# Sixteen rows of x put together in stage 2 instead of transposed in stage 3, another way for the last core plane, and another order of the opening

## The chip, the core and the metric

The kernel runs on one core of one Trainium2 chip. The metric is device time in microseconds (us) of the whole program; three runs of the kernel before gave 3287.86, 3288.17 and 3288.30. Everything is float32. The engines are named as in the profile: PE is TensorE's matrix product and PEld its weight load, DVE is VectorE, ACT is ScalarE, POOL is GpSimd, and SP is SyncE, which here only issues transfers. A float32 product is two passes through TensorE, so a product counts as two PE instructions.

## The reference

A "triangle" layer is followed by a gated layer, on x of 384 x 384 positions (i, j) with 128 channels. Cut to what matters:

```python
z = layernorm(x, norm_g, norm_b)                       # over channels
left  = (z @ Wl + bl) * sigmoid(z @ Wlg + blg)
right = (z @ Wr + br) * sigmoid(z @ Wrg + brg)
core  = einsum('ikh,jkh->ijh', left, right)            # per hidden channel h: a 384x384x384 product
zo    = layernorm(core, onorm_g, onorm_b) @ Wout + bout
x1    = x + sigmoid(x @ Wg + bg) * zo                  # end of layer 0

l   = x1 @ W_left + b_left + x1 @ W_eq + b_eq
rs  = sum over j of (x1 @ W_right + b_right)           # one vector per row i
o   = (l * rs * sigmoid(x1 @ W_gate + b_gate)) @ W_out + b_out
out = layernorm(o + x1, ln_scale, ln_bias)
```

## The kernel before

The work runs in three stages, one after another, with tensors in device memory between them. `seq` keeps all instructions in the order of the program text, so each engine's order is written out by hand.

**Opening (0 to 11 us).** x's first chunk is loaded on SP in two halves with `load_chunk`, the side weights W (128 x 514 with the norm's columns, into `stage`) and their bias row are loaded on ACT's queue. `fold` turns the norm's gain and shift into the weights: `busy(2)` (line 150) issues two products that serve nothing but to occupy TensorE, POOL makes a matrix m1 (lines 159, 160), and for each half of the columns a full product (line 163) and a bias product (line 164), whose operands are one row high (`avg[0:1]`, `brow`), are summed in PSUM. `weights` (line 171, DVE) makes the folded matrix `wz` of it, and `first_step` (line 288) transposes the first rows of normalised x.

**Stage 1 (to 1130 us)** takes x in chunks of 8 rows i by 128 positions k. DVE computes the layer norm's moments, POOL subtracts (`z`, line 262), TensorE transposes (line 271) and multiplies by `wz` (line 323, 128x512), ACT takes the sigmoid (line 332), DVE the product (line 334). Three things go to memory: left and right, by hidden channel, to `lr_d`; the transposed z to `xt_d` (channel, i, block, position); and the subtracted part to `nd_d`. The two sum to x, transposed: x^T of row i is `xt_d[:, i]` plus `nd_d[i]` on every channel.

**Stage 2 (1130 to 1874 us)** is a loop over the 128 hidden channels h. `load_h` brings left and right of one h in two transfers (lines 93 and 94, 768 and 256 KB) into one of three buffers; it is issued for h+3 when TensorE has finished h. `fill(h+1)` copies the right factors to a dense tile `rr` on POOL, one h ahead (lines 468 to 475; the first of the two copies of loaded data, line 474, is 128x768). Nine products (line 493) give three planes of core in PSUM. ACT copies them out (`ct`, line 502) and squares them (line 503), DVE sums both over h (lines 504 and 505) for the second layer norm, and SP stores the planes to `core_d` (line 509, 576 KB). One h takes 5.81 us. The last h has its own sequence: its first plane has a PSUM bank of its own, is copied out first (line 511), stored in two pieces (16 rows and the rest, lines 513 and 514), and the variance, its root (line 425), reciprocal (line 429) and a Newton step (lines 439 to 441) make `r`, the reciprocal deviation for rows 0 to 127. The rest of the planes is copied at line 517 and stored at line 522; POOL's queue stores `r` to `rstd_d` (line 525).

**Stage 3 (1874 to 3287 us)** goes row by row through a written pipeline of steps t. For each row: the gate product `pg` (line 621) and its sigmoid (line 623), the scaled core `cs` (rows 0 to 3 on DVE, line 655, with r spread over the partitions by the product `pb`, line 654; other rows on POOL, line 657, with the loaded `rt`), the product `pr` (line 666), two DVE steps to x1 (lines 667 and 669), two products of layer 1 (lines 683 and 684) with a sigmoid and a product behind them, the output product (lines 695 and 696), the layer norm over channels and the store. All of it needs x transposed. For rows 16 and up, `load_x` reads `nd_d`, spread over the partitions (line 568), and `add_x` adds `xt_d` to it by an accumulating transfer on POOL's queue (line 576). For rows 0 to 15, `load_x` reads x itself (line 562), and `front` transposes each row in three pieces (line 632) and copies it out of PSUM on ACT (line 636) or, for rows 4 to 8, on DVE (line 634); the gate product of a row lags its transposes by L = 4 rows. `load_core` brings core rows in groups of four (line 586); that of the first group is in two transfers, the last 16 channels being the second, and has no `rt`; the others add `rt` (line 590).

SP issues in the order of the text: x of rows 0 to 11, core of rows 0 to 3 (two pieces), x of rows 12 to 15, core and rt of rows 4 to 7, and so on. An issue that waits holds up all that stand behind it in its queue.

Of the kernel before, what the change touches and what calls it, by code (L numbers as in the profile page):

```python
# [8 lines left out]
F32 = mybir.dt.float32  # L9
# [10 lines left out]
def triangle_then_gated_row_kernel(ctx: ExitStack, tc: tile.TileContext, a: dict, out: bass.AP):  # L20
# [9 lines left out]

    nc = tc.nc
    x = a["x"].rearrange("b i j c -> (b i) j c")
    y = out.rearrange("b i j c -> (b i) j c")
# [7 lines left out]
    KEEP = 2  # L43
    RG = 4
    A = 9
    L = 4
    TR = 16

    cpool = ctx.enter_context(tc.tile_pool(name="const", bufs=1))
# [3 lines left out]
    rstd_d = dpool.tile([N, N], F32, name="rstd_d")  # L53
    xt_d = dpool.tile([C, N, NB, P], F32, name="xt_d")
    nd_d = dpool.tile([N, N], F32, name="nd_d")

    def seq(ins):

# [22 lines left out]
    with ExitStack() as ctx2:  # L81
# [17 lines left out]
        with tc.tile_pool(name="p1w", bufs=6, side="right") as wp, \  # L99
# [26 lines left out]
            stage = lrp.tile([P, H, G, 2], F32, tag="lr", name="stage").rearrange("p h i s -> p (h i s)")  # L126

            wst, g0, b0 = stage[:, 0:4 * H], stage[:, 4 * H:4 * H + 1], stage[:, 4 * H + 1:4 * H + 2]
            brow, m1, d = stage[0:1, 5 * H:9 * H], stage[:, 9 * H:10 * H], stage[:, 10 * H:10 * H + 1]
            load(stage[:, 0:4 * H + 2], a["L0_side_W"], nc.scalar)  # L130
            load(brow, a["L0_side_b"].rearrange("(o h) -> o h", o=1), nc.scalar)
            load_chunk(0, slice(4, XR))
            for n in range(1, 4):
                load_chunk(n)
# [1 line left out]
            seq(nc.vector.memset(avg, 1.0 / P))  # L136
            mhalf = const([P, 16], "mhalf")
            seq(nc.vector.memset(mhalf, -0.5))
            ident = const([P, P], "ident")
            make_identity(nc, ident)  # L140

# [5 lines left out]
            def busy(n):  # L147

                for _ in range(n):
                    seq(nc.tensor.matmul(  # L150
                        p0, lhsT=avg, rhs=avg.unsqueeze(1).to_broadcast([P, 4, P]), start=True, stop=True
                    ))

            def fold():

                busy(2)
                seq(nc.gpsimd.tensor_tensor(d, b0, g0, ALU.subtract))
                seq(nc.gpsimd.tensor_tensor(m1, avg, d.to_broadcast([P, P]), ALU.mult))  # L160

                for p, gs in zip((p0, p1), halves):
                    seq(nc.tensor.matmul(p[:, gs], lhsT=m1, rhs=wst[:, gs], start=True, stop=False))
                    seq(nc.tensor.matmul(p[:, gs], lhsT=avg[0:1, :], rhs=brow[:, gs], start=False, stop=True))

            halves = slice(0, 2 * H), slice(2 * H, 4 * H)

# [275 lines left out]
        with tc.tile_pool(name="p2r", bufs=2, side="right", reuse_waits="tile") as rrp, \  # L443
# [14 lines left out]
            def fill(h):  # L458

                if h < H:  # L460
# [15 lines left out]
                    if h == 0:  # L476
                        stay()

            fill(0)
            for h in range(H):  # L480
                fill(h + 1)
                t, rr = loaded2.pop(h), right.pop(h)
                pc = ps.tile([P, NB, 512], F32, tag="pc", name="pc")
                banks = [pc[:, ib, :N] for ib in range(NB)]
                order = [(kb, ib) for kb in range(NB) for ib in range(NB)]
                if h == H - 1:


                    banks[0] = ps1.tile([P, 512], F32, name="pc0")[:, :N]
                    order.sort(key=lambda o: o[1] > 0)  # L490
                    seq(nc.scalar.activation(warm, mhalf[:, 0:1], AF.Sqrt, scale=-1.0))
                for kb, ib in order:
                    seq(nc.tensor.matmul(  # L493
                        banks[ib], lhsT=t[:, kb, ib * P:(ib + 1) * P, 0], rhs=rr[:, kb],
                        start=(kb == 0), stop=(kb == NB - 1),
                    ))

                ct = op.tile([P, NB, N], F32, tag="ct", name="ct")
                sq = qp.tile([P, NB, N], F32, tag="sq", name="sq")
                to = core_d[:, h, :].rearrange("(b p) j -> p b j", p=P)  # L500
                if h < H - 1:
                    seq(nc.scalar.copy(ct, pc[:, :, :N]))  # L502
                    seq(nc.scalar.activation(sq, ct, AF.Square))
                    seq(nc.vector.tensor_add(csum, csum, ct))  # L504
                    seq(nc.vector.tensor_add(csq, csq, sq))
                    load_h(h + 3)

                    queue = nc.sync if h < H - 3 else nc.scalar
                    seq(queue.dma_start(out=to, in_=ct))
                else:  # L510
                    seq(nc.scalar.copy(ct[:, 0], banks[0]))
                    seq(nc.scalar.activation(sq[:, 0], ct[:, 0], AF.Square))
                    seq(nc.scalar.dma_start(out=to[:16, 0], in_=ct[:16, 0]))
                    seq(nc.scalar.dma_start(out=to[16:, 0], in_=ct[16:, 0]))
                    seq(nc.vector.tensor_add(csum[:, 0], csum[:, 0], ct[:, 0]))
# [12 lines left out]
                    seq(nc.gpsimd.tensor_tensor(csq[:, 1:], csq[:, 1:], sq[:, 1:], ALU.add))  # L528
# [5 lines left out]
    with ExitStack() as ctx3:  # L534
# [11 lines left out]
        def work(name, pool=wp):  # L546
            return pool.tile([P, N], F32, tag=name, name=name)

        def work_x(name):

            return lp.tile([P, N], F32, tag="x", name=name)
# [5 lines left out]

        def load_x(i0):

            if i0 < TR:  # L560
                xt = xin[i0] = xp.tile([P, RG, N], F32, tag="xt", name="xn")
                seq(nc.sync.dma_start(
                    out=xt.rearrange("p i (b c) -> p i b c", b=NB),
                    in_=x[i0:i0 + RG].rearrange("i (b p) c -> p i b c", p=P),
                ))
            elif i0 < N:
                xt = xts[i0] = xp.tile([P, RG, N], F32, tag="xt", name="xt")
                seq(nc.sync.dma_start(
                    out=xt.rearrange("p i j -> p (i j)"),
                    in_=nd_d[i0:i0 + RG].rearrange("i j -> (i j)").partition_broadcast(P),  # L570
                ))

        def add_x(i0):
# [7 lines left out]
        def load_core(i0):  # L581
# [33 lines left out]

        def front(f):

            r = rows.get(f - L)
            if r:
                pg = bank("pg")  # L620
                seq(nc.tensor.matmul(pg[:, :N], lhsT=wg0, rhs=r["xT"], start=True, stop=True))  # L621
                gT = r["gT"] = work("gT", fp)
                seq(nc.scalar.activation(gT, pg[:, :N], AF.Sigmoid, bias=bg0))  # L623
            if f < N:
                i0, n = f // RG * RG, f % RG
                if f >= TR:
                    xT = xts[i0][:, n]
                else:
                    xT = work_x("xT")
                    pxt = ps2.tile([P, 512], F32, tag="py", name="pxt") if f < A else bank("pxt")  # L630
                    for s in cols:
                        seq(nc.tensor.transpose(pxt[:, s], xin[i0][:, n, s], ident))
                    if 4 <= f < A:
                        seq(nc.vector.tensor_copy(xT, pxt[:, :N]))
                    else:
# [23 lines left out]
        def layer0(i):  # L659
# [8 lines left out]
            x1T = r["x1T"] = work_x("x1T")  # L668
            seq(nc.vector.scalar_tensor_tensor(
                x1T, pr[:, :N], bout1, r["xT"], ALU.add, ALU.add, accum_out=quad[m]["tot"][:, n:n + 1]  # L670
            ))
# [220 lines left out]
```

## Time and profile before

| what | before |
|---|---|
| three runs, median | 3288.17 us |
| profiled execution, its own time | 3288.61 us |
| its span | 3286.8 us |
| PE busy | 3266.3 us, 99% |
| POOL busy | 2289.6 us, 70% |
| DVE busy | 2491.7 us, 76% |
| ACT busy | 1936.1 us, 59% |
| transfers | 873.70 MB, mean 266 GB/s |

The span runs from the first to the last instruction that the profile shows; the program's own time has some 1.8 us around it. Busy shares are averages over stages that differ: stage 2 and stage 3 each have TensorE busy nearly all the time, while what stands close behind it changes. In rows of the timeline the columns are start, duration, engine, line, operation, tiles and shapes, how many were drawn together, and in brackets how long the engine stood idle before and what released it. In rows of windows they are the stretch and its length, then busy time and instruction count for PE, PEld, DVE, ACT and POOL, then the granted clock of TensorE, the mean busy share of the core's 16 DMA engines, and GB/s.

### The profile page before, as it was taken

The page shows a single profiled execution, that of the slowest core. Times are in us where ns is not written, and L with a number is a line of the kernel's source. Part 1 is how long each engine was busy: PE and PEld are TensorE (multiplying, and loading weights), DVE is VectorE, ACT ScalarE, POOL GpSimd, SP SyncE. Part 2 cuts the span into 40 slices and gives each one's busy share as a digit, 9 for nine tenths or more (in the row PEclk, how much of TensorE's full clock was granted, in tenths as well). Part 3 has the DMA queues.
Part 4 walks back from the last instruction along what each step waited for, and adds up shares of the span by engine and source line. Part 5 has one row for each costly group of instructions (what it writes and reads, how often), then busy time and mean ns, then how long its engine had stood idle before and what let it go on. Part 6 is the DMA issues. An engine that isn't in the chain of part 4 may idle for free.

```text
span 3286.8 us, 48304 instructions
## 1 busy us (share of the span) xinstructions
PE 3266.3 (99%) x12458; PEld 1987.4 (60%) x12458; DVE 2491.7 (76%) x8019; ACT 1936.1 (59%) x4056; POOL 2289.6 (70%) x3299
## 2 busy tenths in 40 slices
PE   9999999999999999999999999999999999999998
PEld 4444444444444566666666666667777777777776
DVE  7777777777777655555555588888888888888888
ACT  4555555555555533333333467677777777777776
POOL 5555555555555466665656578888888888888997
PEclk9999999999999999999999999999999999999999
DMA  6998998999999499999998999999999999999994
GB/s 165 275 280 257 277 281 258 276 280 264 273 279 269 147 280 287 281 282 286 281 282 284 285 294 264 279 281 270 271 280 275 272 273 280 271 272 273 266 254 127
DMA packets 921492, 873.70 MB, mean 266 GB/s; under 512 B 24657, under 2 KB 836177, under 8 KB 921218
## 3 DMA queue, kind: packets, MB, share of 16 engines
q1 hardware_dynamic: 906528, 796.03, 78.2%
q0 software_dynamic: 13312, 72.55, 12.8%
q8 instruction: 102, 1.67, 0.2%
q10 hardware_dynamic: 1378, 2.04, 0.2%
q14 instruction: 172, 1.41, 0.1%
HBM read 508.63 MB, written 361.89 MB: 265 GB/s over the span
## 4 chain that ended last, share of the span: by engine, by line
PE 96%; POOL 2%; ACT 1%; DVE 1%; issue 1%; DMA 0%; POOLq 0%; ACTq 0%; DVEq 0%
PE pr L323 30%; PE pc L493 22%; PE py L695 7%; PE pr L666 7%; PE pl L684 7%; PE pg L621 7%; PE pg L683 7%; PE pt L271 4%; PE py L696 4%; POOL cs L657 1%; POOL rs L715 1%; POOL yt L765 1%; ACT py L730 0%; DMA core_d<-ct 0%; PE pq L643 0%
## 5 line engine op out<-in xcount | busy, mean ns | idle before, releaser
L323 PE MATMUL pr<-wz,zt 128*128 128x512 f32 x2304 | 1040.0, 593 | 0.0
L332 ACT ACTIVATE sg<-pr,rs 128x256 f32<-128x256 f32 x1152 | 483.8, 471 | 496.6 <-PE pr L323 363.3
L493 PE MATMUL pc<-rr,lrh 128*128 128x384 f32 x2304 | 743.3, 486 | 0.3 <-DVE lr L334 0.3
L334 DVE SCALAR_TENSOR_TENSOR lr<-pr,rs,sg 128x256 f32<-128x256 f32 x1152 | 504.7, 480 | 267.4 <-ACT sg L332 218.2
L323 PEld LDWEIGHTS pr<-wz,zt 128*128 128x128 f32 x2304 | 414.2, 190 | 411.0 <-issue 345.9
L493 PEld LDWEIGHTS pc<-rr,lrh 128*128 128x128 f32 x2304 | 452.0, 196 | 291.8 <-issue 1.1
L730 ACT ACTIVATE py<-py,nm,rs 128x128 f32<-128x128 f32 x1149 | 494.4, 431 | 200.2 <-POOL rs L719 122.1
L657 POOL TENSOR_TENSOR cs<-ct,rt 128x384 f32<-128x384 f32 x380 | 427.9, 1130 | 11.2 <-PE pr L666 6.6
L695 PEld LDWEIGHTS py<-wo,u 128*128 128x128 f32 x2304 | 376.6, 191 | 97.5
L504 DVE TENSOR_TENSOR csum<-csum,ct 128x1152 f32<-128x1152 f32 x127 | 179.3, 1412 | 333.5 <-ACT ct L502 333.5
L765 POOL TENSOR_TENSOR yt<-yt,lnb 128x384 f32<-128x384 f32 x380 | 426.0, 1122 | 3.1 <-DVE yt L759 3.1
L502 ACT COPY ct<-pc 128x1152 f32<-128x1152 f32 x127 | 142.2, 1120 | 445.2 <-PE pc L493 436.0
L695 PE MATMUL py<-wo,u 128*128 128x128 f32 x2304 | 402.1, 275 | 0.0
L252 POOL TENSOR_SCALAR sd<-mv 128x8 f32<-128x8 f32 (+1 forms) x145 | 28.7, 198 | 425.2 <-DVE mv L239 425.0
L262 POOL TENSOR_TENSOR z<-xt,nd 128x512 f32<-128x512 f32 x287 | 299.3, 1043 | 34.6 <-POOL z L262 29.4
L710 DVE BATCH_NORM_STATS2 st<-py 128x6 f32<-128x128 f32 x1152 | 265.5, 286 | 66.9 <-PE py L696 65.1
L696 PE MATMUL py<-ident,x1T 128*128 128x128 f32 x1152 | 314.0, 273 | 0.0
L666 PE MATMUL pr<-cs,wc 128*128 128x384 f32 x768 | 313.9, 490 | 0.1
L684 PE MATMUL pl<-x1T,mat_L_conv_W_left 128*128 128x384 f32 x768 | 311.0, 487 | 1.0 <-ACT gT L623 0.9
L683 PE MATMUL pg<-x1T,mat_L_conv_W_gate 128*128 128x384 f32 x768 | 310.8, 486 | 1.1 <-ACT g L686 0.9
L621 PE MATMUL pg<-xt,mat_L_conv_Wg 128*128 128x384 f32 x736 | 298.6, 487 | 1.4 <-ACT gT L623 1.4
L237 DVE BATCH_NORM_STATS2 st<-xt 128x6 f32<-128x128 f32 x1152 | 273.7, 279 | 3.9 <-DMA xt<-in_x_dram 3.9
(127 smaller groups left out, 4819.0 us busy)
## 6 DMA issues: line engine op xcount, KB each, us to landing
lr_d<-lr SPq DMA_DIRECT2D x128, 1024.0 KB, 7.1
lrh<-lr_d SPq DMA_DIRECT2D x128, 768.0 KB, 7.7
xt_d<-zt SPq DMA_DIRECT2D x288, 256.0 KB, 5.4
xt<-in_x_dram SPq DMA_DIRECT2D x143, 512.0 KB, 6.6
ct<-core_d SPq DMA_DIRECT2D x95, 768.0 KB, 6.1
rt<-rstd_d SPq DMA_DIRECT2D x95, 768.0 KB, 7.7
out_dram<-yt SPq DMA_DIRECT2D x94, 768.0 KB, 8.7
core_d<-ct SPq DMA_DIRECT2D x125, 576.0 KB, 8.8
```

The costliest lines, as they stand in the source:

```text
L323: seq(nc.tensor.matmul(pr[:, r, :], lhsT=zts[n, q][:, 2 * half + r, :], rhs=wz, start=True, stop=True))
L332: seq(nc.scalar.activation(sg[r], pr[:, r, 2 * H:], AF.Sigmoid, scale=rs[r]))
L334: seq(nc.vector.scalar_tensor_tensor(t[:, :, c * XR + r0 + r, :], pr[:, r, :2 * H].rearrange("k (h s) -> k h s", s=2), rs[r], sg[r].rearra ...
L493: seq(nc.tensor.matmul(banks[ib], lhsT=t[:, kb, ib * P:(ib + 1) * P, 0], rhs=rr[:, kb], start=(kb == 0), stop=(kb == NB - 1),))
L621: seq(nc.tensor.matmul(pg[:, :N], lhsT=wg0, rhs=r["xT"], start=True, stop=True))
L657: seq(nc.gpsimd.tensor_tensor(cs, ct[:, i % RG], rt[:, i % RG], ALU.mult))
L666: seq(nc.tensor.matmul(pr[:, :N], lhsT=wc, rhs=r["cs"], start=True, stop=True))
L683: seq(nc.tensor.matmul(pg2[:, :N], lhsT=wgate, rhs=r["x1T"], start=True, stop=True))
L684: seq(nc.tensor.matmul(pl[:, :N], lhsT=wleft, rhs=r["x1T"], start=True, stop=True))
L695: seq(nc.tensor.matmul(py[:, s], lhsT=r["u"][:, s], rhs=r["wo"], start=True, stop=False))
L730: seq(nc.scalar.activation(py[:, s], py[:, s], AF.Identity, bias=bias, scale=scale))
L765: seq(engine.tensor_tensor(yt, yt, lnbb, ALU.add))
```

## The change

**Opening.** The side weights move from ACT's queue to SP, between the two halves of x's first chunk. The bias row becomes a full-height tile that DVE sets to zero; its first row is then loaded on ACT's queue. The bias product takes all 128 rows of `avg` and of that tile. `fold` issues one more occupying product, 128 columns wide.

**Stage 2.** `early_x` makes x^T of rows 0 to 15, one row every five steps of h, in three transfers several steps apart: SP loads `nd_d[i]` over the partitions to a tile, POOL's queue adds `xt_d[:, i]` to it, SP stores it to a new tensor `xf_d`. The first plane of the last h is copied to a tile of its own, `last_h`, and stored by one transfer.

**Stage 3.** `load_x` reads `xf_d` for rows 0 to 15. The transposes, their copies, and the lag L are gone: `front` issues the gate product of a row at once, from another PSUM pool for some of the first rows, and runs ahead by a rule of its own. For rows 0 to 3 the core of the last h comes by four direct transfers from `last_h`, and the second piece of that core load covers channels 111 to 126, so that it doesn't need the last plane in memory; x of rows 8 to 11 is loaded after the first piece, and core of rows 4 to 7 ahead of x of rows 12 to 15. Sizes of three pools change.

```diff
-            brow, m1, d = stage[0:1, 5 * H:9 * H], stage[:, 9 * H:10 * H], stage[:, 10 * H:10 * H + 1]
-            load(stage[:, 0:4 * H + 2], a["L0_side_W"], nc.scalar)
-            load(brow, a["L0_side_b"].rearrange("(o h) -> o h", o=1), nc.scalar)
+            brow, m1, d = stage[:, 5 * H:9 * H], stage[:, 9 * H:10 * H], stage[:, 10 * H:10 * H + 1]
+            load(stage[:, 0:4 * H + 2], a["L0_side_W"])
             load_chunk(0, slice(4, XR))
...
+            seq(nc.vector.memset(brow, 0.0))
+            load(brow[0:1], a["L0_side_b"].rearrange("(o h) -> o h", o=1), nc.scalar)
...
                 busy(2)
+                busy(1, 1)
...
-                    seq(nc.tensor.matmul(p[:, gs], lhsT=avg[0:1, :], rhs=brow[:, gs], start=False, stop=True))
+                    seq(nc.tensor.matmul(p[:, gs], lhsT=avg, rhs=brow[:, gs], start=False, stop=True))
...
+            def early_x(h):
+                for n, step in enumerate((6, 8, 11)):
+                    i, odd = divmod(h - step, 5)
+                    if not odd and 0 <= i < TR:
+                        if n == 0:
+                            early[i] = rp.tile([P, N], F32, tag="ve", name="xe", bufs=NB)
+                            seq(nc.sync.dma_start(out=early[i], in_=nd_d[i].partition_broadcast(P)))
+                        elif n == 1:
+                            seq(nc.gpsimd.dma_start(
+                                out=early[i], in_=xt_d[:, i].rearrange("c b k -> c (b k)"), accum_op=ALU.add
+                            ))
+                        else:
+                            seq(nc.sync.dma_start(out=xf_d[:, i], in_=early.pop(i)))
...
                 fill(h + 1)
+                early_x(h)
...
-                    seq(nc.scalar.copy(ct[:, 0], banks[0]))
-                    seq(nc.scalar.activation(sq[:, 0], ct[:, 0], AF.Square))
-                    seq(nc.scalar.dma_start(out=to[:16, 0], in_=ct[:16, 0]))
-                    seq(nc.scalar.dma_start(out=to[16:, 0], in_=ct[16:, 0]))
+                    seq(nc.scalar.copy(last_h, banks[0]))
+                    seq(nc.scalar.activation(sq[:, 0], last_h, AF.Square))
+                    seq(nc.scalar.dma_start(out=to[:, 0], in_=last_h))
...
-        xp, lp, fp, inp = pool("p3x", 6), pool("p3l", 20), pool("p3f", A), pool("p3in", 3)
-        wp, sp, op, up = pool("p3w", 4), pool("p3s", 4), pool("p3out", 3), pool("p3u", 18)
+        xp, lp, fp, inp = pool("p3x", 6), pool("p3l", 18), pool("p3f", A + 3), pool("p3in", 3)
+        wp, sp, op, up = pool("p3w", 4), pool("p3s", 4), pool("p3out", 3), pool("p3u", 17)
...
-                for hs in (slice(0, H),) if i0 > 0 else (slice(0, H - 16), slice(H - 16, H)):
+                for hs in (slice(0, H),) if i0 > 0 else (slice(0, H - 16), slice(H - 17, H - 1)):
                     seq(nc.sync.dma_start(out=ct[hs], in_=core_d[i0:i0 + RG, hs].rearrange("i h j -> h i j")))
+                    if between and hs.start == 0:
+                        between()
+                        for i in range(RG):
+                            seq(nc.sync.dma_start(out=ct[H - 1:H, i], in_=last_h[i:i + 1]))
...
-                    for s in cols:
-                        seq(nc.tensor.transpose(pxt[:, s], xin[i0][:, n, s], ident))
-                    if 4 <= f < A:
-                        seq(nc.vector.tensor_copy(xT, pxt[:, :N]))
-                    else:
-                        seq(nc.scalar.copy(xT, pxt[:, :N]))
-                rows[f] = {"xT": xT}
+            r = rows[f] = {"xT": xts[f // RG * RG][:, f % RG]}
+            pg = ps2.tile([P, 512], F32, tag="py", name="pg") if f < A and f % 2 == 0 else bank("pg")
+            seq(nc.tensor.matmul(pg[:, :N], lhsT=wg0, rhs=r["xT"], start=True, stop=True))
...
-        for i0 in range(0, 3 * RG, RG):
-            load_x(i0)
-        load_core(0)
+        load_x(0)
+        load_x(RG)
+        load_core(0, between=lambda: load_x(2 * RG))
+        load_core(RG)
         load_x(3 * RG)
-        load_core(RG)
...
-            while f < min(N + L, t + max(L, A - t // 3)):
+            while f < min(N, t + max(1, A - t // 2)):
                 front(f)
                 f += 1
...
-            if t >= 2 and fetched <= f + 16:
+            if t >= 2 and fetched <= t + 18:
```

More of the change, by code (lines that the diff above doesn't have):

```diff
@@ L45, in triangle_then_gated_row_kernel @@
     A = 9
-    L = 4
     TR = 16
@@ L55, in triangle_then_gated_row_kernel @@
     nd_d = dpool.tile([N, N], F32, name="nd_d")
+    xf_d = dpool.tile([C, TR, N], F32, name="xf_d")
     def seq(ins):
@@ L145, in triangle_then_gated_row_kernel, with busy @@
             p0, p1 = (pps.tile([P, 2, 4 * H], F32, tag="pr", name=n)[:, 0] for n in ("p0", "p1"))
-            def busy(n):
+            def busy(n, cols=4):
                 for _ in range(n):
                     seq(nc.tensor.matmul(
-                        p0, lhsT=avg, rhs=avg.unsqueeze(1).to_broadcast([P, 4, P]), start=True, stop=True
+                        p0[:, :cols * P], lhsT=avg, rhs=avg.unsqueeze(1).to_broadcast([P, cols, P]),
+                        start=True, stop=True,
                     ))
@@ L477, in fill @@
                         stay()
+            def early_x(h):
[11 more added lines that the diff above has]
+                            seq(nc.sync.dma_start(out=xf_d[:, i], in_=early.pop(i)))
+            early = {}
+            last_h = rp.tile([P, N], F32, tag="r", name="last_h", bufs=NB)
             fill(0)
@@ L510, in triangle_then_gated_row_kernel @@
                 else:
-                    seq(nc.scalar.copy(ct[:, 0], banks[0]))
-                    seq(nc.scalar.activation(sq[:, 0], ct[:, 0], AF.Square))
-                    seq(nc.scalar.dma_start(out=to[:16, 0], in_=ct[:16, 0]))
-                    seq(nc.scalar.dma_start(out=to[16:, 0], in_=ct[16:, 0]))
-                    seq(nc.vector.tensor_add(csum[:, 0], csum[:, 0], ct[:, 0]))
+                    seq(nc.scalar.copy(last_h, banks[0]))
+                    seq(nc.scalar.activation(sq[:, 0], last_h, AF.Square))
+                    seq(nc.scalar.dma_start(out=to[:, 0], in_=last_h))
+                    seq(nc.vector.tensor_add(csum[:, 0], csum[:, 0], last_h))
                     seq(nc.vector.tensor_add(csq[:, 0], csq[:, 0], sq[:, 0]))
@@ L547, in work @@
             return pool.tile([P, N], F32, tag=name, name=name)
-        def work_x(name):
-            return lp.tile([P, N], F32, tag="x", name=name)
         cols = [slice(b * P, (b + 1) * P) for b in range(NB)]
@@ L558, in load_x @@
         def load_x(i0):
[L560 to L566, printed above, removed]
+            if i0 < N:
                 xt = xts[i0] = xp.tile([P, RG, N], F32, tag="xt", name="xt")
@@ L569, in load_x @@
                     out=xt.rearrange("p i j -> p (i j)"),
-                    in_=nd_d[i0:i0 + RG].rearrange("i j -> (i j)").partition_broadcast(P),
+                    in_=xf_d[:, i0:i0 + RG].rearrange("c i j -> c (i j)") if i0 < TR
+                    else nd_d[i0:i0 + RG].rearrange("i j -> (i j)").partition_broadcast(P),
                 ))
@@ L579, in add_x, with load_core @@
                 ))
-        def load_core(i0):
+        def load_core(i0, between=None):
             if i0 < N:
                 ct = inp.tile([P, RG, N], F32, tag="ct", name="ct")
-                for hs in (slice(0, H),) if i0 > 0 else (slice(0, H - 16), slice(H - 16, H)):
+                for hs in (slice(0, H),) if i0 > 0 else (slice(0, H - 16), slice(H - 17, H - 1)):
                     seq(nc.sync.dma_start(out=ct[hs], in_=core_d[i0:i0 + RG, hs].rearrange("i h j -> h i j")))
+                    if between and hs.start == 0:
+                        between()
+                        for i in range(RG):
+                            seq(nc.sync.dma_start(out=ct[H - 1:H, i], in_=last_h[i:i + 1]))
                 rt = None
@@ L616, in front @@
         def front(f):
[L618 to L627, printed above, removed]
-                else:
-                    xT = work_x("xT")
-                    pxt = ps2.tile([P, 512], F32, tag="py", name="pxt") if f < A else bank("pxt")
-                    for s in cols:
-                        seq(nc.tensor.transpose(pxt[:, s], xin[i0][:, n, s], ident))
-                    if 4 <= f < A:
-                        seq(nc.vector.tensor_copy(xT, pxt[:, :N]))
-                    else:
-                        seq(nc.scalar.copy(xT, pxt[:, :N]))
-                rows[f] = {"xT": xT}
+            r = rows[f] = {"xT": xts[f // RG * RG][:, f % RG]}
+            pg = ps2.tile([P, 512], F32, tag="py", name="pg") if f < A and f % 2 == 0 else bank("pg")
+            seq(nc.tensor.matmul(pg[:, :N], lhsT=wg0, rhs=r["xT"], start=True, stop=True))
+            gT = r["gT"] = work("gT", fp)
+            seq(nc.scalar.activation(gT, pg[:, :N], AF.Sigmoid, bias=bg0))
         def right_sums(i0, i1):
@@ L667, in layer0 @@
             seq(nc.vector.scalar_tensor_tensor(pr[:, :N], pr[:, :N], bz, r["gT"], ALU.add, ALU.mult))
-            x1T = r["x1T"] = work_x("x1T")
+            x1T = r["x1T"] = work("x1T", lp)
             seq(nc.vector.scalar_tensor_tensor(
```

## The prediction

> **What bounds the kernel now.** I read the engine totals and the chain that ended last first, then windows of each stage, then the timeline at the two places that the diff opens up (the kernel's first 15 us, and the seam from stage 2 to stage 3), and last the waits inside stage 2.
>
> ```profile
> span 3286.8 us, 48304 instructions
> PE 3266.3 (99%) x12458; PEld 1987.4 (60%) x12458; DVE 2491.7 (76%) x8019; ACT 1936.1 (59%) x4056; POOL 2289.6 (70%) x3299
> ...
> PE 96%; POOL 2%; ACT 1%; DVE 1%; issue 1%; DMA 0%; POOLq 0%; ACTq 0%; DVEq 0%
> ```
>
> TensorE is the bound from end to end: 20.5 us of the span lie outside its work, and the chain is 96% TensorE. Only three things can move the time: less TensorE work, TensorE work at a better clock, or gaps between its products, filled or opened. The windows (PE busy is the second figure; the last three are granted clock, DMA share, GB/s) say where there are gaps and where the cover is thin:
>
> ```profile
> 0.00:15.00 15.00, 13.38 (x23) 5.67 (x24) 8.09 (x51) 2.92 (x6) 8.60 (x21) 1.00 0.77 196
> 1165.00:1600.00 435.00, 435.00 (x1350) 264.63 (x1350) 237.72 (x150) 171.28 (x150) 270.65 (x449) 1.00 0.91 283
> 1874.00:1895.00 21.00, 19.96 (x86) 12.52 (x85) 15.71 (x29) 12.14 (x23) 9.66 (x8) 1.00 0.96 306
> 1895.00:1930.00 35.00, 35.00 (x152) 23.39 (x151) 28.21 (x89) 19.45 (x43) 17.92 (x25) 1.00 0.93 311
> ```
>
> Stage 2 (second row) has no PE gap at all, but its 16 DMA engines are busy 0.91 of the time. The seam (third row) has little to fill. So the change takes work from TensorE in stage 3 and hands DMA work to a stage that has little room.
>
> **Part 1, transposes and copies of rows 0 to 15 (stage 3).**
>
> ```profile
> L632 PE MATMUL pxt<-ident,xn x48: 272/273/329, 1874.0 to 1905.7; 128*128 128x128 f32 x48
> ...
> 1878.01 0.49 PE L632 MATMUL pxt<-ident,xn 128*128 128x128 f32 x3
> 1878.34 0.81 PE L621 MATMUL pg<-xT,mat_L_conv_Wg 128*128 128x384 f32 x2
> ```
>
> The 273 ns of one transpose overlap their neighbours: three begin at 1878.01 and the gate product behind them at 1878.34, so a row's three cost 0.33 us. 16 rows x 0.33 = 5.3 us of TensorE work go, and all of it lay on the bounding engine. The 16 copies that emptied them go too (11 of 0.47 us on ACT, 5 of 0.55 us on DVE). Their time was off the path except at one place:
>
> ```profile
> 1879.54 0.56 DVE L441 SCALAR_TENSOR_TENSOR r<-r,m 128x384 f32<-128x384 f32 x1
> 1880.02 2.50 DVE L634 COPY xT<-pxt 128x384 f32<-128x384 f32 x5
> 1882.69 0.56 DVE L655 TENSOR_TENSOR cs<-ct,pb 128x384 f32<-128x384 f32 x1 [0.17 <-PE pb L654]
> ```
>
> Five copies stand between the finished r and the first scaled core row cs. Without them and without transposes I replay TensorE's order from 1873.98: nine gate products at 0.645 us (starts of successive products, 1879.31 to 1879.96) end at 1879.8; pb of row 0 follows r (1880.1); cs needs pb and its core rows. Row 0's second core piece landed at 1882.57 before (issued 1877.65, 4.92 us). It is now issued at about 1879.5, because it also waits for the direct copies' sources and for the store of the last plane's rest (issued 1875.27; it took 6.74 us before, I take 4 to 5 with fewer transfers in flight), and is a sixteenth of a transfer that took 4.9, so it lands about 1882 if that goes well. Then pr of row 0 starts near 1882.9 (1885.65 before) and pr of row 4 near 1891.3: 26 products x 0.645 = 16.8 us from 1874.0 plus 0.5 idle. Before it was 1895.13, with nine gate products done where the new order has twelve. So at that point 3.8 us plus 3 x 0.645 = 1.9 us are won, and the remaining transposes (three rows or so, 1.0 us) come after: 6.7. The direct sum agrees: 5.3 of transposes and some 1.5 of the 2.0 us that TensorE idles between 1874 and 1895.13. I take **-6.5** (-7.2 to -2.5; the small end is the rival below in which the store is late). The four one-row copies, the move of the third x load behind the first core piece and the core load of rows 4 to 7 ahead of x of rows 12 to 15 cost SP about 0.4 us of issue each. Behind them on SP stand rt of rows 4 to 7 and the later loads; rt waits for rstd in memory, which before landed at 1886.6 and let rt go only at 1886.65, so SP has cover until then.
>
> **Part 2, x of those rows made in stage 2.** Per row, every fifth h: a 192 KB load of nd (SP), a 192 KB accumulating transfer (GpSimd), a 192 KB store (SP): 32 more issues on SP, 16 on GpSimd. SP issues 1.2 us of transfers per h of 5.81, so the issues are covered. GpSimd has 35 to 40% idle here (270.65 of 435 us busy), so 16 issues of about 0.9 us are covered too, unless they fall just before the copies that feed TensorE. The transfers' own time is what counts:
>
> ```profile
> POOL rr L474 <- DMA lrh<-lr_d: 85.2, 62, 2.2
> ...
> 1505.41 1.77 POOL L474 COPY rr<-lrh 128x768 f32<-128x768 f32 x1 [2.04 <-DMA lrh<-lr_d]
> ...
> DMA to landing us min/median/max: 4.6/7.7/9.3
> ```
>
> GpSimd's copy of the next h's right factors waited for the 768 KB load (L93, whose times to landing are the last line) in 62 of 75 steps: the landing already sets when rr is ready. It is ready 1.3 to 2.6 us before TensorE needs it (the copy shown ends at 1507.2; the h before it ends at 1508.5), so a landing may slip from 7.7 to some 10 us after issue at no cost; beyond that each us is a us of TensorE.
>
> Rule against row: the Trainium skill, "DMA: Bandwidth & Descriptors", section "Issuing engines are not separate DMA queues", says that transfers from SP, ACT and GpSimd run on the same 16 engines and interleave, so using GpSimd's queue buys issue time only. By that, add 2.2 us per row on each engine: 0.52 (load) + 1.16 (accumulate, at the 173 GB/s that 72.55 MB in 12.8% of the span make) + 0.52 (store), all estimates from this trace's rates. Idle is 0.09 x 5.81 x 5 = 2.6 us per five steps. 2.2 fits into 2.6, so on even engines the cost is 0; share 0.91 would become 0.99. But the engines aren't even: in the load's packets 12 or 13 of 16 engines finish near 4.5 us after the issue and the rest at 7 to 8.5, and this lag shrinks by only some 0.2 us per step. By that row, 2.2 - 5 x 0.2 = 1.2 us per row stay in the slow engines' queues; after two rows the 2.3 us of slack are gone, and 14 x 1.2 = 17 us would reach TensorE. Between 0 and +17 I take **+0.6**, near the rule's sum, because the lag shrinks faster once it is above 8.5 us; the upper end is the first rival.
>
> **Part 3, the opening.**
>
> ```profile
> 1.05 3.78 PE L150 MATMUL p<-avg 128*128 128x512 f32 x4 [1.05 <-DVE mhalf L138]
> 5.36 1.22 PE L163 MATMUL p<-stage 128*128 128x256 f32 x2 [0.53 <-POOL stage L160]
> 6.51 1.22 PE L164 MATMUL p<-stage,avg 1*128 1x256 f32 x2
> ...
> 11.11 3.96 PE L323 MATMUL pr<-wz,zt 128*128 128x512 f32 x6
> 15.34 2.82 PE L323 MATMUL pr<-wz,zt 128*128 128x512 f32 x6
> ```
>
> Passes of 512 take 0.95 us at first, 0.43 later, though the clock column shows 1.00 throughout; the change to the fast pace falls inside the six at 11.11. Two bias products (one row high) become full height, an extra small product fills part of the 0.53 us gap, W moves behind x's first half on SP, and the bias load waits for a memset (0.5 us DVE, in DVE's 3.93 us wait for x).
>
> Rule against row: the skill's "TensorE: Matmul & The Clock Gate", Part 1, has a cold TensorE run at half speed until about 3.4 us of one free-running window were busy. Taken simply that would have come at 4.5 us; the row shows half speed 9 us longer, behind the gap and the low products. If the fuller opening satisfies it one or two windows earlier, the four fold products (4.6 us) and the first passes speed up: the two waits of DVE for them (0.94 and 1.21 us) fall away and up to 2.0 us are won, where GpSimd's z of the next step becomes the limit. By the row alone (3.78 us unbroken did not suffice) the gain is 0, and W landing later on SP (4.55 before) costs up to 0.4. I take **-1.6** (-2.0 to +0.4), the end that a product train without a low or empty stretch is nearer to.
>
> **Sum.** -6.5 + 0.6 - 1.6 = -7.5 on the profiled execution of 3288.61 us (span 3286.8 and 1.8 around it) = 3281.1; the median of the three runs is 0.44 below it, so **3280.7**. Own range of this case: -9.7 to -4.7, 3278.5 to 3283.5.
>
> **Rivals.**
> (a) DMA backlog in stage 2. For: 62 waits of 75, share 0.91 before any addition. Against: it fits on average, and a landing has 2.3 us of slack. With the 17 us above, net -8.1 + 17 = +9: **3297**. Slower than before from 8.1 us of stall (0.5 us per row), beyond the measurable bound of 6.6 us (0.2%) from 15 us (0.9 per row).
> (b) Core rows late. If the store of the last plane's rest lands as late as before (1882.01), the second core piece is issued then and lands at 1885 to 1887; TensorE runs out of gate products and pb at about 1883 and idles 2 to 4 us. Stage 3 gains 2.5 to 3 and the sum is -3.7: **3284.5**. For: that store took 6.7 us. Against: half of its company in the queue is gone.
> (c) The clock rises no earlier. The opening gains nothing: **3282.3**, just short of a measurable gain.
> (d) The saved 5.3 us are given back later, because GpSimd or ACT limit rows 16 on. Against: 2400 to 2800 has PE busy 399.98 of 400. 3280.7 + 5.3 = **3286**.
>
> **How the numbers follow.** Forecast 0.50, (c) 0.14, (b) 0.14, (d) 0.05, (a) 0.17 with everything from 3286 to 3300. Differences under 0.2% (6.6 us) can't be told from no change by this measurement. Faster by more (below 3281.6): 0.36 of the forecast's 0.50, half of (c), which centres close to that bound: 0.43. Slower by more (above 3294.7): the upper four fifths of (a), 0.14. Same: 0.43. The range 3278 to 3292 leaves out 0.05 below and 0.15 above.
>
> **What the new profile would show.** L632, L634, L636 gone; first row's pr at about 1882.9 minus the opening's gain; the opening's first L323 near 10.2 and its six passes below 3 us; in stage 2 PE busy 100% with the 62 waits grown in length, not in their effect, DMA share near 0.99. PE idle of more than 0.1 us per h in 1200 to 1600 would be (a); a cs that waits for DMA beyond 1883, (b); passes at 0.9 us until 13, (c).

## The result and the profile after

The changed kernel takes 3282.62 us (median of 22 runs, 3281.32 to 3285.37) against 3288.25 us before (22 runs, 3286.81 to 3289.53): a ratio of 0.9984 with a 95% interval of 0.9978 to 0.9989, or 5.6 us less. The forecast was 3280.7, 7.5 us less. The interval leaves out 1, so the change is real. At 0.17% it is just under the 0.2% that the prediction takes as the smallest gain it can tell from none.

The profiled execution took 3283.63 us, 4.98 less than that of before. Line numbers are those of each run's own kernel. First the page, then the windows of the stages (PE busy is the second figure, DMA share and GB/s the last two):

```profile
span 3281.9 us, 48294 instructions
PE 3257.4 (99%) x12412; PEld 1981.6 (60%) x12412; DVE 2486.3 (76%) x8015; ACT 1929.0 (59%) x4045; POOL 2287.3 (70%) x3315
...
PE 91%; POOL 5%; issue 1%; ACT 1%; DVE 1%; DMA 0%; SPq 0%; POOLq 0%; DVEq 0%; ACTq 0%
```

```profile
0.00:15.00 15.00, 12.53 (x34) 6.11 (x34) 9.90 (x58) 4.49 (x9) 9.29 (x24) 1.00 0.87 233
1165.00:1600.00 435.00, 435.00 (x1351) 264.63 (x1350) 239.09 (x150) 170.89 (x150) 276.12 (x465) 1.00 0.98 303
1870.00:1892.00 22.00, 19.44 (x60) 10.87 (x59) 14.87 (x28) 11.38 (x21) 8.21 (x7) 1.00 0.86 284
```

TensorE lost 9 us of busy time, the span only 4.9, and the chain that ended last has 91% on TensorE instead of 96%. Stage 2's part (1165 to 1600) still has TensorE busy throughout, at a DMA share of 0.98 instead of 0.91. The seam has more idle than before: 2.6 of 22 us, against 1.0 of 21.

Read as marks on TensorE, before minus after: stage 2 begins at 1130.86 and 1128.70 (-2.16) and its products end at 1874.14 and 1871.98 (-2.16, so stage 2 itself costs nothing). From there to DVE's last instruction it takes 1406.37 and 1402.67 (-3.70). From that instruction to the end of the span it is 6.32 and 7.20 (+0.88). The sum is -4.98. These are two single profiles. In five others of the old stages 2 and 3, stage 2's end to DVE's last instruction takes 1405.5 to 1405.6 (that of the recorded profile, 1406.4, was 0.8 long), so -2.9 is the better figure for stage 3.

The opening on TensorE, after:

```profile
1.05 4.15 PE L153 MATMUL p<-avg 128*128 128x512 f32 x6 [1.05 <-DVE avg L136]
5.83 0.70 PE L168 MATMUL p<-stage 128*128 128x256 f32 x2 [0.64 <-POOL stage L165]
6.37 0.59 PE L169 MATMUL p<-stage,avg 128*128 128x256 f32 x2
...
9.37 2.84 PE L328 MATMUL pr<-wz,zt 128*128 128x512 f32 x6
```

The fold's pairs now take 0.43 to 0.54 us from start to start, not 1.15, and the six passes behind them 2.84 instead of 3.96. The clock column says 1.00 all along, as before.

The seam. Before, row 0's `pr` on TensorE, and the two pieces of the first core load on SP (in SP's rows the duration runs from the first to the last of the issues drawn together):

```profile
1885.65 0.81 PE L666 MATMUL pr<-cs,wc 128*128 128x384 f32 x2
...
1870.94 7.03 SPq L586 DMA_DIRECT2D ct<-core_d  x2
```

After, on DVE, TensorE and SP:

```profile
1877.37 0.56 DVE L446 SCALAR_TENSOR_TENSOR r<-r,m 128x384 f32<-128x384 f32 x1
1882.59 1.49 DVE L662 TENSOR_TENSOR cs<-ct,pb 128x384 f32<-128x384 f32 x3 [4.66 <-DMA ct<-core_d]
...
1883.20 0.91 PE L673 MATMUL pr<-cs,wc 128*128 128x384 f32 x2 [2.30 <-DVE cs L662]
...
1872.02 7.30 SPq L607 DMA_DIRECT2D ct<-last_h  x4
1879.42 1.62 SPq L603 DMA_DIRECT2D ct<-core_d  x2
```

r is ready at 1877.9, but DVE waits 4.66 us for the core rows, and TensorE 2.30 us for cs. Those rows were issued at 1879.42, behind four small copies that took SP 7.3 us to issue. For the first 5.5 us of these SP waits for the store of channel 126, which the rows need too; it lands at 1877.52. From then on the copies alone hold the rows up, for 1.9 us.

### The profile page after: what moved, and what is told of

Same layout as the page of the kernel before. It is cut to its first block, busy times and chain, and to the rows that moved or that the text cites. A ratio compares the mean times of both kernels' runs of the same rounds, so it can differ in the third digit from the quotient of the medians.

```text
span 3281.9 us, 48294 instructions
## 1 busy us (share of the span) xinstructions
PE 3257.4 (99%) x12412; PEld 1981.6 (60%) x12412; DVE 2486.3 (76%) x8015; ACT 1929.0 (59%) x4045; POOL 2287.3 (70%) x3315
## 4 chain that ended last, share of the span: by engine, by line
PE 91%; POOL 5%; issue 1%; ACT 1%; DVE 1%; DMA 0%; SPq 0%; POOLq 0%; DVEq 0%; ACTq 0%
PE pr L328 30%; PE pc L518 22%; PE py L702 6%; PE pr L673 6%; PE pl L691 6%; PE pg L690 6%; PE pg L642 6%; PE pt L276 4%; PE py L703 3%; POOL rs L722 1%; POOL yt L772 1%; POOL cs L664 1%; ACT py L737 1%; DMA core_d<-ct 0%; POOL nm L725 0%
## 5 line engine op out<-in xcount | busy, mean ns | idle before, releaser
L664 POOL TENSOR_TENSOR cs<-ct,rt 128x384 f32<-128x384 f32 x380 | 425.7, 1126 | 11.5 <-DMA rt<-rstd_d 5.9
L642 PE MATMUL pg<-xt,mat_L_conv_Wg 128*128 128x384 f32 x768 | 310.5, 487 | 1.8 <-ACT gT L644 1.6
L479 POOL COPY rr<-lrh 128x768 f32<-128x768 f32 x128 | 178.5, 1394 | 170.6 <-DMA lrh<-lr_d 170.4
```

The source lines that it names most:

```text
L664: seq(nc.gpsimd.tensor_tensor(cs, ct[:, i % RG], rt[:, i % RG], ALU.mult))
```

## The experiments

Medians are compared with runs of the kernel before on the same chip, since that kernel's own median was 3289.2 us on one chip and 3288.2 to 3288.3 on the others.

**The new opening alone.** The kernel before with the changed kernel's opening:

```diff
-            load(stage[:, 0:4 * H + 2], a["L0_side_W"], nc.scalar)
-            load(brow, a["L0_side_b"].rearrange("(o h) -> o h", o=1), nc.scalar)
+            load(stage[:, 0:4 * H + 2], a["L0_side_W"])
...
+            seq(nc.vector.memset(brow, 0.0))
+            load(brow[0:1], a["L0_side_b"].rearrange("(o h) -> o h", o=1), nc.scalar)
...
+                busy(1, 1)
...
-  ... matmul(p[:, gs], lhsT=avg[0:1, :], rhs=brow[:, gs], ...)
+  ... matmul(p[:, gs], lhsT=avg, rhs=brow[:, gs], ...)
```

> The kernel before with the new opening alone (x first, W on SP, full-height bias product, extra small product); stages 2 and 3 as before. If the whole 2.2 us by which the changed kernel enters stage 2 earlier comes from the opening, this run starts stage 2 near 1128.7 us instead of 1130.9, and is 2.2 us faster than before (3286.0). If a part of it is chance of the clock's phase in one profiled run, the median is less than 1.5 us faster. What it leaves of the changed kernel's 5.6 us is then stage 3's share: 3.4 us, not the 6.5 forecast.

Measured: 3285.97 against 3289.20 us, ratio 0.999 (0.9983 to 0.9996). Its stage 2 starts at 1128.06, 2.8 us earlier than before, even 0.6 earlier than in the changed kernel's profile. There W landed late: POOL's first step on W began at 5.11 us, here at 4.45. This profile is of the fastest of the kernel's 20 runs. By the medians the opening is worth about 3 us (1.3 to 5.6 by the interval), more than half of the whole change.

**Which part of the opening.** Three kernels undo one part in the changed kernel, three more make one part alone in the kernel before, and one is the kernel before again.

```diff
# changed kernel, no extra product
-                busy(1, 1)
# changed kernel, bias product one row high
-  ... matmul(p[:, gs], lhsT=avg, rhs=brow[:, gs], ...)
+  ... matmul(p[:, gs], lhsT=avg[0:1, :], rhs=brow[0:1, gs], ...)
# changed kernel, W back on ACT's queue
-            load(stage[:, 0:4 * H + 2], a["L0_side_W"])
+            load(stage[:, 0:4 * H + 2], a["L0_side_W"], nc.scalar)
# kernel before with each part alone: one hunk of the diff above at a time
# (height: the memset, the bias load and the product); and unaltered
```

> The changed kernel without the extra small occupying product. Theory 1 (TensorE's train of products up to 5.2 us is what brings the fast pace by 6.1 us): without it the train ends at 4.8 us, the pace stays slow through the fold, and the kernel is 1 to 2 us slower than changed (3284 to 3285). Rival (the height of the bias product, or loads' order, is what counts): no more than 0.5 us slower.

> The changed kernel with the bias product one row high again. In the changed kernel's trace the pace is fast from about 6.1 us, before the first bias product. Theory 1 (the train ahead of it decides): same time as changed, 3282.6 within 0.5. Rival (the height decides, as the change's name has it): the fold's four products take 4.6 us again and the kernel is about 2 us slower (3284.7).

> The changed kernel with W back on ACT's queue, beside both halves of x's first chunk. Theory 1: W lands 0.4 us earlier, x's first half 1.3 us later; the fast pace still comes before the fold; POOL's z becomes the limit, so 0.3 to 1 us slower than changed. Rival (the order of the loads makes the whole gain): about 2 us slower (3284.7).

> The kernel before, unaltered, for a second profile of its opening. If the late rise of TensorE's pace (13.4 us) belongs to the program, it comes near 13.4 again and stage 2 starts at 1130.9 within 0.3. If it is chance of a window's phase, it may come at 5 to 10 us here, and then stage 2 starts up to 2 us earlier.

> The kernel before with only the extra small product. It closes the gap before the fold to about 0.1 us. Theory 1 (an unbroken train of full-height products until about 6.5 us raises the pace by then): pace fast by 6.7 us although the bias products are still one row high, stage 2 starts 1 to 2 us earlier, time 1 to 2 us below before. Rival (one-row bias products keep it slow): pace slow until 13, same time as before within 0.3 us.

> The kernel before with only the full-height bias products. The gap of 0.5 us before the fold stays, but the fold is a full train of 4.6 us. Theory 1: fast by 10 us at the latest, 1 to 2 us below before. Rival (only the train ahead of the fold counts): slow until 13, same as before.

> The kernel before with only the loads' order (x's first half ahead, W on SP). Theory 1: the gap before the fold grows or stays, the bias products are low, the pace stays slow until about 13; z is ready earlier but TensorE isn't; same as before within 0.5 us. Rival (the order of loads makes the gain): 2 us or more below before.

Measured, in us. "Fast" is a start every 0.2 to 0.33 us for a pass of 256 columns in the fold and every 0.43 us for a pass of 512; "slow" is 0.4 to 0.6 and 0.85. The first projection product is the first with `wz`. The last column is the difference of the medians on the same chip; its 95% interval is 2 to 3 us either way.

| kernel | fold's pace | first projection product | its first passes | stage 2 starts | against before |
|---|---|---|---|---|---|
| before | slow | 11.11 | slow to 13.6 | 1130.86 | |
| before, again | slow | 11.08 | slow to 13.8 | 1131.05 | +0.3 |
| before + extra product | fast from 6.4 | 9.96 | slow to 13.3 | 1130.09 | -1.3 |
| before + full height | fast | 9.87 | fast | 1129.20 | -2.1 |
| before + loads' order | fast | 8.96 | slow to 12.1 | 1128.89 | -1.9 |
| before + all three | fast from 7.0 | 8.86 | fast | 1128.06 | -3.2 |
| changed | fast | 9.37 | fast | 1128.70 | -5.6 |
| changed, no extra product | fast | 9.08 | fast | 1128.30 | -6.0 |
| changed, one-row bias | fast from 6.2 | 8.98 | fast | 1128.09 | -5.4 |
| changed, W on ACT | fast from 6.3 | 9.82 | fast | 1129.16 | -4.3 |

The single parts' ratios have intervals that reach just over 1 (0.9986 to 1.0004 and the like). So they rest on the traces, one of each kernel, where the starts of single instructions are on record. The theory that the train of products ahead of the fold decides (theory 1) fails twice: without the extra product nothing is lost, and the order alone gains 1.9 us where none was expected. For the full height alone it held. Three things follow.

First, the order of the loads has a worth of its own that isn't the clock. With x's first half ahead, DVE starts its moments at 3.5 to 3.8 us instead of 4.9 to 5.0, so POOL's z comes 0.5 to 1.3 us earlier. Every kernel with the new order starts its projection by 9.4, every fast one without it at 9.8 to 10.0. With W on ACT and with the full-height product alone, TensorE stands 1.1 and 1.6 us waiting for z.

Second, each part alone was enough to make the fold fast, but only full height also kept the pace. TensorE's rows of the kernel before with only the loads' order:

```profile
5.27 0.70 PE L163 MATMUL p<-stage 128*128 128x256 f32 x2 [0.44 <-POOL stage L160]
5.90 0.69 PE L164 MATMUL p<-stage,avg 1*128 1x256 f32 x2
...
8.96 4.13 PE L323 MATMUL pr<-wz,zt 128*128 128x512 f32 x6
```

The fold is fast from 5.27, yet the six passes take 4.13 us: the pace has fallen again, as it has in the kernel with only the extra product. Both have the one-row bias products and idle or transposes after them. With full height it did not fall in any profile, nor with one-row products where the two other parts were in.

Third, what raises the pace isn't settled. Ahead of the fold TensorE starts the same four passes, within 0.02 us, in the two profiles of before and in those with only the order or only the height. The fold was slow in the first two and fast in the others. So what TensorE did before does not decide it alone, and no run here shows what else does. The unprofiled runs add one thing. With full height alone 11 of 12 runs lie within 0.5 us of each other, with all three parts 18 of 20 within 0.6; with the order alone the runs spread over 4.3 us, those of before on the same chip over 3.8. From stage 2 on, the profiles of these kernels agree within 0.1 us in all but one, so the spread is probably the opening's and full height steadies it. That is not shown, as no kernel's opening was profiled in many runs.

**The direct copies: order, and undone.** In the traces, the transfers of SP and ACT take eight completion counters (semaphores) in turn, and one that gets a counter goes only when the transfer that had it before has landed. The first copy goes at 1872.02, 0.06 us after the store of channel 125 landed, the second at 1877.54, 0.02 us after that of channel 126; each has that store's counter. The copies read neither store.

```diff
# the second core piece ahead of the copies
                 for hs in ...:
                     seq(nc.sync.dma_start(out=ct[hs], in_=core_d[i0:i0 + RG, hs]...))
                     if between and hs.start == 0:
                         between()
-                        for i in range(RG):
-                            seq(nc.sync.dma_start(out=ct[H - 1:H, i], in_=last_h[i:i + 1]))
+                if between:
+                    for i in range(RG):
+                        seq(nc.sync.dma_start(out=ct[H - 1:H, i], in_=last_h[i:i + 1]))
# the last plane as before
-                    seq(nc.scalar.copy(last_h, banks[0]))
-                    seq(nc.scalar.dma_start(out=to[:, 0], in_=last_h))
+                    seq(nc.scalar.copy(ct[:, 0], banks[0]))
+                    seq(nc.scalar.dma_start(out=to[:16, 0], in_=ct[:16, 0]))
+                    seq(nc.scalar.dma_start(out=to[16:, 0], in_=ct[16:, 0]))
...
-  ... (slice(0, H - 16), slice(H - 17, H - 1))      # and no copies
+  ... (slice(0, H - 16), slice(H - 16, H))
```

> The changed kernel with the second core piece of rows 0 to 3 issued ahead of the four direct copies. Theory 2 (the counters of transfers' completions, eight used in turn, make the copies wait on SP for unrelated stores, and the core piece behind them in the queue with them: 1872.0 to 1879.4): the piece is then held only by the store of channel 126 (landed 1877.5), goes at 1877.6 and lands near 1880.6; cs of row 0 moves from 1882.6 to about 1880.8, TensorE's 2.3 us of idle shrink to 0.5, and the kernel is 1.5 to 1.9 us faster than changed (3281). Rival (DMA bandwidth sets the landing whatever the order): the piece lands at 1882 all the same, change within 0.4 us.

> The changed kernel with the last plane as before: no direct copies, stored in two pieces (16 rows and the rest) and loaded with the second core piece. Theory 2: the piece waits for the stores of channel 126 (1877.5) and of the 16 rows (about 1876), so it goes at 1877.6, 1.9 us earlier than with the copies in front of it: 1 to 2 us faster than changed. Rival (the direct copies save a trip through memory): the 16 rows' store comes later, row 0's core after 1883, 1 us or more slower than changed.

Measured for the order: 3280.95 us (3280.45 to 3281.95) against 3288.17, ratio 0.998 (0.9972 to 0.9988). Two kernels with the changed kernel's stage 3 (below), run on the same chip, have medians of 3282.67 and 3282.55, and 31 of their 40 runs are slower than the slowest here. So 1.6 to 1.7 us come from the order of five transfers. SP and TensorE in it:

```profile
1875.62 0.32 SPq L603 DMA_DIRECT2D ct<-core_d  x1
1875.98 2.46 SPq L608 DMA_DIRECT2D ct<-last_h  x4
...
1880.19 0.81 PE L674 MATMUL pr<-cs,wc 128*128 128x384 f32 x2
```

The piece goes at 1875.62, 0.08 us after channel 126's store landed, and lands 2.33 us later. TensorE has no wait in front of pr, which comes 8.75 us after stage 2's last product. Of the 2.5 us that pr gains on the changed kernel's profile, 1.4 are not the order's: that store landed 4.1 us after stage 2's last product here and 5.5 there. In the five other profiles with the changed seam it landed after 3.8 to 4.8 us, and the piece went 1.9 to 2.8 us behind it. That delay is what the order removes. TensorE's idle time at the seam falls from 2.56 to 0.69 us. What is left is a wait of row 2's core for its copy (1.2 us on DVE), since copies three and four now land at 1881.4 and 1881.9.

Measured with the last plane as before: 3282.33 us, ratio 0.9983 (0.9976 to 0.9989), as fast as changed, not the 1 to 2 us faster expected. Its core piece does go at 1876.20 and lands at 1878.50, but now r is late. The wait on ACT:

```profile
ACT ct L535 <- DMA core_d<-ct: 1.8, 1, 1.8
```

Without `last_h` the last plane is copied to a buffer that an earlier store still reads. Counted from stage 2's last product, r is ready 1.9 us later than in the changed kernel, and the copy of the other planes starts 1.1 us later. So by these traces the tile of its own is the useful half of this part of the change, and the four copies in front of the core piece are the costly half; the tile alone was not run.

**More transfers in stage 2.** The changed kernel with its sixteen rows made every third and every second h:

```diff
-                    i, odd = divmod(h - step, 5)
+                    i, odd = divmod(h - step, 3)     # and 2 in the other kernel
```

> The changed kernel with the rows of x made every third h instead of every fifth (16 rows in 48 steps): 0.73 us of extra transfer time per engine and step against 0.52 us idle. Theory 3 (the 16 DMA engines are what gives way, idle time is usable to the last tenth): excess 0.21 x 48 = 10 us less the 2.3 us of slack: stage 2 is 5 to 8 us longer than 743.1. Rival (there is more room than the busy share shows, transfers speed up when they overlap): stage 2 stays at 743.1 within 1 us.

> The same with every second h (16 rows in 32 steps): 1.1 us of extra transfer time per engine and step against 0.52 idle. Theory 3: excess 0.58 x 32 = 18.6 us less 2.3: stage 2 some 14 to 17 us longer. Rival: under 5 us longer.

Measured: 3282.67 and 3282.55 us (ratio 0.9984 both, 0.9977 to 0.9990 and 0.9977 to 0.9991), the changed kernel's time. Stage 2 from its first product to its last takes 743.28 us in the second, as in the kernel before. The window that holds its transfers, at every second h:

```profile
1165.00:1340.00 175.00, 175.00 (x544) 106.54 (x543) 95.97 (x62) 68.76 (x61) 117.05 (x195) 1.00 1.01 329
```

and the same window before:

```profile
1165.00:1340.00 175.00, 175.00 (x544) 106.42 (x544) 94.01 (x60) 68.53 (x60) 110.12 (x180) 1.00 0.92 284
```

The share stands at its full value, the engines move 16% more bytes, and TensorE misses nothing. Theory 3 is refuted at two and a half times the change's load. In these windows SP's queue moved 54.6 MB at a share of 0.888, where before 49.6 MB took 0.914: less engine time on record carried more. The 768 KB loads that fill rr landed in 7.8 us (median) and 8.6 (longest) before in this window, in 7.8 and 8.8 in the changed kernel, in 8.1 and 8.6 here.

## Why the prediction was right, and where it was not

The sign and the range held: 3282.6 lies in 3278 to 3292, 1.9 us above the point. On the size class the forecast was undecided: it gave "faster by more than 0.2%" and "within 0.2%" 0.43 each, with its point in the first; the second came. That it came so close is luck in part: stage 2 and the opening came out 0.6 and about 1.2 us better than their terms, stage 3 and the end of the program 3.6 and 0.9 us worse.

**Stage 2 (+0.6 taken, 0 to +17 bounded): 0.0.** The choice near the rule of the Trainium skill's "DMA: Bandwidth & Descriptors", section "Issuing engines are not separate DMA queues", was the better one, and the row set against it was misread twice. The waits of POOL for the load did become more, as said:

```profile
POOL rr L479 <- DMA lrh<-lr_d: 100.8, 72, 2.8
```

That is 72 waits instead of 62 in 1165 to 1600, without effect on TensorE. But a busy share of 0.91 was taken as 0.91 of what can be moved; at a share of 1.01 the engines moved 329 GB/s against 284, and SP's queue carried 13% more bytes per unit of share, so the time that packets are on record stretches when there is room. And the lag of the slow engines was taken as a queue that adds up. The landings of two and a half times the load show that it doesn't. Rival (a) falls. (One figure in the sum is too low: 0.52 us for 192 KB is 378 GB/s, while SP's queue moved 796.03 MB in 78.2% of the span of before, 310 GB/s. At that rate the 2.2 us per row are 2.4.)

**Opening (-1.6 taken, -2.0 to +0.4): -2.2 in the profile, -2.7 to -3.0 in the five others with the same opening, -3.2 by the medians of the opening alone.** The mechanism taken from the Trainium skill's "TensorE: Matmul & The Clock Gate", Part 1, holds in its direction: with the fuller train of products the pace was fast sooner, by 5.8 us instead of 13.6. The bound of -2.0 failed because it took POOL's z as fixed. The very step that was priced only as "W landing later" brings x's first half 1.3 us earlier (DVE's first moments at 3.67 instead of 4.95), and with it z. Of the order of loads only the cost was counted. Rival (c) falls: in all twelve profiles that have one of the three parts or more, the fold is fast by its second half.

**Transposes (-5.3): right.** 48 passes fewer, and TensorE's rows are otherwise the same. From stage 2's last product to its own last product TensorE is busy for 1388.4 us, against 1393.6 with the opening alone (whose stages 2 and 3 are those of before): 5.2 less. It stands idle for 6.6 us there, against 4.4. So stage 3 gains 5.2 and loses 2.3, where the forecast had a further 1.5 us of gain.

**The seam: the step that failed.** "It is now issued at about 1879.5 ... so it lands about 1882" came true on the clock on the wall (1879.42, 1882.41), but by luck. It was reckoned from a stage 2 that ends at 1874.14, and stage 2 ended 2.16 us earlier. Counted from stage 2's last product, the piece was to go after 5.4 us and went after 7.4, and pr of row 0 was forecast at 8.8 us and came at 11.2.

What was mis-sized is the wait for the stores ahead of the piece. The forecast names that of the last planes' rest, and takes 4 to 5 us for it "with fewer transfers in flight"; it took 5.87, and landed 0.5 us before the piece went. It puts the store of channel 126 at nothing. That store is issued 4.61 us before stage 2's last product in all fourteen profiles. It took 10.15 us here and 6.46 before, and landed 5.5 us after that product instead of 1.9. In front of it stood 3 MB of x and core loads; the first core load goes 8.6 us before stage 2's end in the new order, 3.2 before. Over the profiles the early core load and the slow store go together (7.5 to 10.1 us in the eight new ones, 6.0 to 7.1 in the six old), but that one causes the other was not tested alone. The copies then add 1.9 us; the forecast had priced them at 0.4 us of issue each and not at the counters that they wait for.

So TensorE's idle time at the seam did not fall by 1.5 us but rose: in the windows from 1.0 to 2.6 us. (The forecast's 2.0 us before are not in its own window, which shows 21.00 - 19.96 = 1.04; they come from counting each product at the distance of two starts, and by that count idle time up to pr of row 4 rose from about 2 to about 3.) That is the size of rival (b), 2.5 to 3 us of gain in stage 3, and also its kind, core rows late; its store was the wrong one. The experiment that moves the piece ahead of the copies brings pr of row 0 to the forecast's 8.8 us and gets 1.6 us back, nearly half of what the step was short.

A smaller part of the shortfall is rival (d). Counted at equal numbers of gate products, stage 3 leads that of the opening alone by 3.8 us at row 16 and by 2.9 at its end; with the order of transfers changed it is 5.6 and 4.3. So 0.9 to 1.2 us are given back after row 16, and why is open.

**The tail, in no part of the forecast: +0.88.** Both kernels end with one addition on DVE and a last store. Before:

```profile
3279.78 0.74 DVE L765 TENSOR_TENSOR yt<-yt,lnb 128x384 f32<-128x384 f32 x1
```

After:

```profile
3273.91 0.75 DVE L772 TENSOR_TENSOR yt<-yt,lnb 128x384 f32<-128x384 f32 x1
```

Their ends are 6.32 and 7.20 us from the end of the span. That pair of values is the same to 0.01 us in all fourteen profiles: 6.32 in the six with the old stages 2 and 3, 7.20 in the eight with the new. In those compared in detail, POOL's final drain ends 1.3 us later after DVE's last instruction (6.4 us instead of 5.1). Why is open; the 16 more transfers of POOL's queue were not taken away alone.

With the other five profiles of the old stage 3, stage 3 gives -2.9 and the tail +0.9: -2.0 net against -6.5 forecast, and the opening -2.8 against -1.6.

## What to carry to other kernels

Reckon the times at the start of a stage from the end of the one before it, and each event from its own releaser: a time that agrees on the wall clock can hide two errors that cancel, as 2.2 us and 2.1 us did here. When loads move ahead of stores that someone waits for, price those stores anew. Issue what the critical instruction needs ahead of the small transfers beside it on one queue, and look which completions each of them waits for, also by way of shared counters. A DMA busy share near 1 says that packets are on record, not that no more bytes fit: raise the load and look at the landings.

## What was not expected of the hardware

- DMA engines at a share of 0.92 moved 284 GB/s, at 1.01 they moved 329 GB/s, with landing times of the transfers that mattered within 0.3 us (medians of 7.8 and 8.1).
- TensorE's pace can fall again within 2 us of work. With the order alone, fold passes start every 0.31 us until 7.5 us, then passes of 512 every 0.86 us from 9.0 to 11.5, with the clock column at 1.00.
- A fold that alternates one-row and full-height products takes 0.31 to 0.32 us for a pass of either kind at the fast pace, and 0.22 where all are full height. So a part of what the height saves need not be the clock.
- The end of the program, after the last instruction of DVE, took 6.32 or 7.20 us, fixed by the kernel and not by the run.
